# Statistics of two tiles at a time, biases carried in the weights' last row, and one gelu per block in a four-layer kernel

## The chip, the cores and the metric

The kernel runs on one core of a Trainium2 chip. The metric is device time in microseconds (us) for one launch; before the change it is 726.42 us, the median of three runs (725.71 to 728.25). A core has five engines that run their own instruction streams and wait for each other through semaphores: TensorE (PE in the profile, its weight loads PEld), VectorE (DVE), ScalarE (ACT), GpSimd (POOL) and SyncE (SP), which here only issues transfers.

## The reference

The input `u` has 8 sequences of 512 tokens with 128 features. Four layers follow each other, each on a layer norm without gain and bias, each added to its input:

```
x = x + L0_attn(ln(x))   # state-space scan; W_in, W_out divided by max(largest singular value, 1)
x = x + L0_ffn(ln(x))    # ln(x) @ W[idx] + b[idx], idx = argmax(log_softmax(logits) + gumbel(u))
x = x + L1_attn(ln(x))   # delta rule: 16 heads of 8 x 8 state, step by step over the tokens
x = x + L1_ffn(ln(x))    # experts

def L1_ffn(x, w_router, w1, b1, w2, b2):
    probs = softmax(x @ w_router)
    topk_w, topk_idx = top_k(probs, 2)          # two of eight experts
    h = gelu(x @ w1[i] + b1[i])                 # 128 -> 512, tanh form
    out = sum over the two of weight * (h @ w2[i] + b2[i])
```

All numbers are float32. A layer norm's output `(x - mean) / sqrt(var + eps)` sums to zero over the 128 features; the change makes use of it.

## The kernel before

The 4096 tokens are cut into 32 tiles of 128 rows (16 steps of each of the 8 sequences), and the tiles into eight groups of four (`SIZES`). For each group `first_layers` computes the scan (`scanned`, `ssm_out`) and the second layer (`linear`), `delta_in` the projections of the third layer, `delta_rule` its recurrence, and `route` the choice of experts. The experts run on bundles of 4, 8, 8, 8 and 4 tiles (`GROUPS`): `experts` sorts the tokens by expert with indexed transfers of GpSimd (`scatter`, line 1233, into `places`), reads them back in blocks of 128 rows (15 blocks for a bundle of 4 tiles, 23 for one of 8, 99 in all), applies both products of the block's expert, writes `results`, and gathers them back by index (line 1368).

`delta_rule` has four steps per tile, and each step six VectorE instructions that depend on one another (lines 1023 to 1037): a product over `kq`, a reduction of `so`, a product and a reduction with `tmat`, a product into `st` and its reduction, which is the state of the next step. `kq` is loaded by SP from DRAM (`scratch`), where `delta_in` has put q and k.

At the start `spectral` finds the largest singular values of `W_in` and `W_out` by squaring a matrix 24 times (two matrices side by side), with a scale from the trace at every third squaring; the results make `gain`, which `ssm_out` needs.

The places in the code that the change and the prediction touch:

- `moments` (line 722): for each tile a statistics instruction on VectorE (`bn_stats`, six numbers: count, mean and sum of squared deviations of the even elements and of the odd ones) and one that joins them (`bn_aggr`). It is called for the input (`input_statistics`, tile names ending in i) and in `linear` (a), `delta_in` (b) and `route` (e). `factors` (732) makes `rstd` and `shift` from it on GpSimd, with a power; `normalised` (749) applies them on ScalarE.
- `linear` (875): `x1b = x1 + bsel` on GpSimd, then `x2 = product + x1b` on VectorE. `wsel` and `bsel`, the chosen weights and bias, come by indexed transfers (710 to 719).
- `w1b_dram` (656 to 663): the experts' first weights with four more columns that hold the biases, made in DRAM by one transfer of `w1` and one of the columns; `rows` (509) gathers small vectors, the 32 rows of `b1` among them, which TensorE transposes into `cols`.
- `hidden_of` (1310): loads a block's weights (`load_weights`, 1274), four products into one PSUM bank (`ph`, two banks), and four gelus of 128 columns, each with its bias column.

Nothing is issued in the order of the text. `Recorder` notes every operation (so line 317 stands in the profile for nearly all), and `Plan.best` (184) works out an order for all engines by list scheduling: an operation gets a key (`nc.key`, in estimated us; `due(t)` is 15 t), a cost from `_cost` and a wait from `LAG`; `place` (210) starts on each engine, among the operations that are ready within 0.7 us, the one with the lowest rank, which is its key or, in a second turn, its latest start worked back from the end (`backward`). An operation that is ready while the engine has nothing else is started, however late its key. The order with the earliest estimated end among `DRAFTS` drafts with randomly moved keys is then issued; on the chip each engine follows it strictly. SP's transfers are among these operations: one that waits holds those behind it. Memory is handed out in turn: `ptile(shape, tag, bufs)` gives the next of a tag's buffers, so `"w1b"` (five buffers) serves `x` of the later groups at first and the experts' weights afterwards, and `"hid"` (three) the raw weights and then the hidden blocks.

Of the kernel before, what the change touches and what calls it, by code (L numbers as in the profile page):

```python
# [17 lines left out]
P = 128  # L18
# [6 lines left out]
NHB = 4  # L25
SQUARINGS = 24
FIRST = 9
# [313 lines left out]
def _cost(engine, name, n, kw):  # L341

    if engine == "tensor":
        return 0.2 if name == "transpose" else 0.22 + 0.0019 * max(_size(kw["rhs"])[1] - 96, 0)
    if engine == "vector":
        if name == "tensor_tensor_scan":
            return 0.1 + 0.0026 * n
        return 0.19 + 0.00103 * n + (0.2 if n == 9 * 32 else 0.0)
    if engine == "scalar":
        columns = sum(isinstance(kw.get(k), bass.AP) for k in ("bias", "scale"))  # L350
        return 0.18 + 0.00085 * n + (0.0, 0.0001 * n, 0.13)[columns]
    return 0.22 + 0.0015 * n if n < 64 else 0.4 + 0.0017 * n

# [3 lines left out]
BEHIND = 8.0  # L357
DRAFTS = 60
JITTER = 15
# [7 lines left out]
def seq_kernel(  # L367
# [72 lines left out]
    def ctile(shape, name, dtype=F32):  # L440
        return const.tile(shape, dtype, tag=name, name=name)
# [18 lines left out]

    WIDE = {"both": 2 * N, "xne": P, "w1b": NHB * P + NHB, "drive": N + B, "z": N + B, "kq": NR * QN, "prod": B * BL * BL}

# [4 lines left out]
    def stile(shape, tag, dtype=F32, bufs=2):  # L467
        return turn(
            "small_" + tag, bufs, lambda name: pipe.tile(shape, dtype, tag=name, name=name)
        )[tuple(slice(0, m) for m in shape)]  # L470
# [35 lines left out]

    R_BP, R_AL, R_DB, R_G, R_B, R_QKVB, R_B1 = 0, 3, 4, 5, 6, 7, 11
    n_rows = R_B1 + NE * NHB
    rows = ptile([n_rows, P], "hid", 3)
    nc.scalar.dma_start(rows[R_BP : R_BP + 3], bp.rearrange("(c p) -> c p", p=P))  # L510
    for r, v in ((R_AL, alpha_log), (R_DB, delta_bias), (R_G, ln_g), (R_B, ln_b)):
        nc.scalar.dma_start(rows[r : r + 1], v.rearrange("(c p) -> c p", p=P))
    nc.scalar.dma_start(rows[R_QKVB : R_QKVB + 4], b_qkvb.rearrange("(c p) -> c p", p=P))
    nc.scalar.dma_start(rows[R_B1:], b1.rearrange("e (c p) -> (e c) p", p=P))
    lg_col = ctile([P, 1], "lg_col")
# [10 lines left out]
    wr = ctile([P, NE], "wr")  # L526
    nc.sync.dma_start(wr, w_router)

    b2_sb = ctile([NT * NE, NT, D], "b2_sb")
# [122 lines left out]
    def col(r):  # L652
        return cols[:, r : r + 1]


    FW = NHB * P + NHB
    w1b_dram = dram.tile([NE * P, FW], F32, tag="w1b_dram", name="w1b_dram")
    nc.key = 0.0
    nc.sync.dma_start(w1b_dram[:, 0 : NHB * P], w1.rearrange("e d f -> (e d) f"))
    nc.sync.dma_start(  # L660
        w1b_dram[:, NHB * P :].rearrange("(e p) c -> p e c", p=P),
        cols[:, R_B1:].rearrange("p (e c) -> p e c", c=NHB),
    )

# [39 lines left out]
    w_row = ctile([P, 1], "w_row", U32)  # L704
    nc.vector.tensor_copy(w_row, pk[:, 4:5])
    b_row = ctile([P, 1], "b_row", U32)
    nc.vector.tensor_copy(b_row, topi[:, 0:1])
    wsel = ctile([P, D], "wsel")
    bsel = ctile([P, D], "bsel")
    for dst, src, row in (  # L710
        (wsel, ffn_W.rearrange("e d f -> (e d) f"), w_row),
        (bsel, ffn_b, b_row),
    ):
        nc.gpsimd.indirect_dma_start(
            out=dst[:, :],
            out_offset=None,
            in_=src,
            in_offset=bass.IndirectOffsetOnAxis(ap=row[:, :1], axis=0),
        )


    def moments(src, part, bufs=2):

        n = src.shape[1]
        st = stile([P, NT, 6], "st" + part)
        mv = stile([P, NT, 2], "mv" + part, F32, bufs)[:, 0:n]
        for i in range(n):
            nc.vector.bn_stats(st[:, i, :], src[:, i, :])
            nc.vector.bn_aggr(mv[:, i, :], st[:, i, :])
        return mv  # L730

    def factors(mv, part, norms=1, bufs=2):

        n = mv.shape[1]
        rstd = stile([P, norms, NT], "rstd" + part, F32, bufs)[:, :, 0:n]
        nc.gpsimd.tensor_scalar_add(rstd[:, 0], mv[:, :, 1], LN_EPS)
        if norms == 2:

            nc.gpsimd.tensor_scalar(rstd[:, 1], mv[:, :, 1], 1.0 + LN_EPS, LN_EPS * LN_EPS, ALU.mult, ALU.add)
        nc.gpsimd.tensor_tensor(rstd, rstd, mhalf[:, 0:norms, 0:n], ALU.pow)  # L740
        shift = stile([P, norms, NT], "shift" + part, F32, bufs)[:, :, 0:n]
        nc.gpsimd.tensor_mul(shift, mv[:, :, 0].unsqueeze(1).to_broadcast([P, norms, n]), rstd)
        nc.gpsimd.tensor_scalar_mul(shift, shift, -1.0)
        return rstd, shift
# [3 lines left out]

    def normalised(src, rstd, shift, xn, norm=0):
        for i in range(src.shape[1]):  # L750
            nc.scalar.activation(
                xn[i], src[:, i, :], AF.Identity, bias=shift[:, norm, i : i + 1], scale=rstd[:, norm, i : i + 1]
            )
        return xn

    def tiles_of(v):
        return [v[:, i, :] for i in range(v.shape[1])]
# [22 lines left out]
    def over_tiles(v, n):  # L780
        return v.unsqueeze(1).to_broadcast([P, n, D])
# [93 lines left out]
    def linear(x1):  # L875

        n = x1.shape[1]
        rstd, shift = statistics(x1, "a")
        xT = ptile([P, n * P], "f", FIRST)
        nc.scalar.copy(xT, transposed(normalised(x1, rstd, shift, tiles_of(ptile([P, n, D], "f", FIRST)))))  # L880
        x1b = ptile([P, n, D], "f", FIRST)
        nc.gpsimd.tensor_add(x1b, x1, over_tiles(bsel, n))
        x2 = ptile([P, n, D], "x2", 2)
        nc.vector.tensor_add(x2, tokens_out(xT, wsel), x1b)
        return x2
# [178 lines left out]
    def route(g, x3, group):  # L1064
# [3 lines left out]
        rstd, shift = statistics(x3, "e")  # L1068
        x3n = normalised(x3, rstd, shift, [ptile([P, D], "xne", MAXT) for _ in range(NT)])
        x3T = ptile([P, N], "x3T")  # L1070
# [94 lines left out]
    def experts(group):  # L1165
# [144 lines left out]
        def hidden_of(j):  # L1310
# [16 lines left out]
            for c in range(NHB):  # L1327
# [3 lines left out]
                )  # L1331
            for c in range(NHB):
                cs = slice(c * P, (c + 1) * P)
                nc.scalar.activation(
                    hid[:, cs], ph[:, cs], AF.Gelu_apprx_tanh, bias=w1b[:, NHB * P + c : NHB * P + c + 1]
                )
            return hid
# [66 lines left out]
    sp = ctile([P, 24], "sp")  # L1404
    smax, rmax, rtr, sums, lam, sig = (sp[:, i : i + 2] for i in (0, 2, 6, 8, 12, 14))
    nc.vector.tensor_reduce(smax, w_both, AX.X, ALU.max, apply_absolute_value=True)
# [13 lines left out]
    def spectral(i, copied, scaled):  # L1420

        c = slice(i, i + 1)
        junk = ptile([P, P], ("x3T", "fin")[i])

        def power():
            return ptile([P, P], ("xbT", "xne")[i], (2, MAXT)[i])

        def total(x, y, column):

            sums_ = part[:, 2 * column + i : 2 * column + i + 1]  # L1430
            if x is y:
                nc.scalar.activation(junk, x, AF.Square, accum_out=sums_)
            else:
                nc.vector.tensor_mul(junk, x, y)
                nc.vector.tensor_reduce(sums_, junk, AX.X, ALU.add)
            at = ph_tile()[:, 0:1]
            nc.tensor.matmul(
                at, lhsT=ones, rhs=part[:, 2 * column + i : 2 * column + i + 1], start=True, stop=True
            )
            return at  # L1440

        cur, a0 = power(), ptile([P, P], f"back{i}")
        scaled(cur, w_both[:, i, :], rmax[:, c])
        factor = None
        for step in range(SQUARINGS + 1):
            bank = po_tile()
            nc.tensor.matmul(bank[:, 0:P], lhsT=cur, rhs=cur, start=True, stop=True)
            if step % 3 == 0 and step < SQUARINGS:


                trace = total(cur, cur, 0)
                nc.vector.tensor_scalar_max(rtr[:, c], trace, 1e-18)
                nc.vector.reciprocal(rtr[:, c], rtr[:, c])
                nc.vector.tensor_mul(rtr[:, c], rtr[:, c], rtr[:, c])
            cur = a0 if step == 0 else power()
            if step % 3 == 1:
                scaled(cur, bank[:, 0:P], rtr[:, c])
            else:
                copied(cur, bank[:, 0:P])
            yield  # L1460
        nc.vector.tensor_copy(sums[:, c], total(cur, a0, 0))
        nc.vector.tensor_scalar_max(rtr[:, c], total(cur, ident, 1), TINY)
        nc.vector.reciprocal(rtr[:, c], rtr[:, c])
        yield

# [3 lines left out]
    for _ in zip(  # L1469
        spectral(0, nc.vector.tensor_copy, vector_scaled), spectral(1, nc.scalar.copy, nc.scalar.mul)  # L1470
    ):
        pass
    nc.vector.tensor_mul(lam, sums, rtr)
    nc.gpsimd.tensor_tensor(sig, lam, half, ALU.pow)
# [23 lines left out]
    for g in range(1, NG):  # L1498
# [4 lines left out]
        input_statistics(g, x)  # L1503

    x2s = {g: first_layers(g) for g in range(2)}
    for g in range(NG):
# [70 lines left out]
```

## Time and profile before

| | |
|---|---|
| median of three runs | 726.42 us |
| the profiled execution | 728.65 us |
| its span, first to last instruction | 726.9 us |
| mean granted TensorE clock | 0.832 |
| first step of the delta rule (`so`) | 105.35 us |
| first gelu of an expert block | 276.4 us |
| last bundle's places known (`dest`) | 642 us |
| last expert product on TensorE | 707.2 us |
| DMA traffic | 105.94 MB, 146 GB/s |

The page of the profile lists busy time by engine. As stages with different limits follow each other, tables by stretches of 20 us say more. Groups of instructions carry the names of the tiles they write and read (`out<-in`), their shape, count, busy time, mean duration, and the idle time ahead of them with what ended it. The page names DRAM tensors by their ends.

### The profile page before, as it was taken

Reading aid. Unit: us, or ns where it says so; the run is one execution under the profiler, and the core shown is the slowest. Engines: PE = TensorE matmul, PEld = TensorE weight load, DVE = VectorE, ACT = ScalarE, POOL = GpSimd, SP = SyncE. Lnnn points to the kernel's source line nnn. Section 1 sums busy time; section 2 is a strip of 40 time slices with the busy share of each in tenths; the row PEclk is TensorE's granted clock in tenths of the full one; section 3 lists DMA queues with packets and bytes.
Section 4 is the critical chain, followed back from the end, with each engine's and each line's share of the span. In section 5 each row is a group of like instructions: output and inputs, shape, how many; then the busy total and the mean of one; then the engine's idle time right before and its main releaser. Section 6 shows DMA issues by size and latency. Waiting matters only on the chain. (4 is left out here: it accounts for less than half of the span.)

```text
span 726.9 us, 11166 instructions
## 1 busy us (share of the span) xinstructions
PE 520.2 (72%) x2948; PEld 403.9 (56%) x2948; DVE 527.0 (73%) x1468; ACT 468.8 (64%) x1062; POOL 548.1 (75%) x681
## 2 busy tenths in 40 slices
PE   5885466576584288699558788883978887988890
PEld 4672124435353156368326577662857776888890
DVE  5775068998999799999959999995798998230013
ACT  3865747654692679998675987852675743675560
POOL 6667485694768899699868998978478878876454
PEclk9856566877699599889758889996899999999995
DMA  3734263233352564276456456565686786569662
GB/s 106 200 108 123 60 148 79 73 95 88 78 125 75 143 178 125 76 181 179 127 148 162 111 138 169 163 173 135 168 211 184 201 245 194 171 192 276 168 176 80
DMA packets 97717, 105.94 MB, mean 146 GB/s; under 512 B 9100, under 2 KB 72535, under 8 KB 97655
## 3 DMA queue, kind: packets, MB, share of 16 engines
q1 hardware_dynamic: 92992, 96.66, 49.2%
q0 software_dynamic: 4160, 8.53, 4.0%
q8 instruction: 25, 0.41, 0.3%
q14 instruction: 38, 0.30, 0.1%
q10 hardware_dynamic: 502, 0.03, 0.0%
HBM read 81.26 MB, written 23.94 MB: 145 GB/s over the span
## 5 line engine op out<-in xcount | busy, mean ns | idle before, releaser
L317 ACT ACTIVATE hid<-ph,w1b 128x128 f32<-128x128 f32 x396 | 113.4, 378 | 48.7 <-PE ph L317 23.4
L317 PE MATMUL ph<-xbT,w1b 128*128 128x128 f32 x792 | 118.3, 292 | 12.0 <-DMA w1b<-w1b_dram 5.4
L317 PEld LDWEIGHTS ph<-xbT,w1b 128*128 128x128 f32 x792 | 107.3, 205 | 26.4 <-issue 10.7
L317 DVE TENSOR_TENSOR so<-kq,st 128x512 f32<-128x512 f32 x128 | 87.5, 684 | 15.6 <-PE in L317 7.9
L317 POOL DMA_INDIRECT back<-results,small_dest x64 | 62.8, 982 | 33.0 <-issue 14.0
L317 DVE TENSOR_REDUCE st<-so 128x32 f32<-128x288 f32 x128 | 84.1, 657 | 3.5
L1297 PE MATMUL po<-w_sb,hid 128*128 x536 | 80.3, 288 | 7.2 <-ACT hid L317 4.0
L1297 PEld LDWEIGHTS po<-w_sb,hid 128*128 128x128 f32 x536 | 73.2, 204 | 15.7 <-issue 7.3
L1235 POOL DMA_INDIRECT places<-xne,small_dest x64 | 64.3, 1004 | 18.8 <-issue 13.7
L286 ACT ACT_TABLE_LOAD x52 | 66.7, 1283 | 6.2 <-DMA hid<-in_L_ffn_b_dram 5.4
L317 PE MATMUL po<-wo,so 128*128 128x128 f32 x256 | 45.0, 330 | 32.9 <-DVE so L317 14.8
L317 DVE TENSOR_REDUCE st<-st 128x64 f32<-128x320 f32 x128 | 63.6, 497 | 4.0
L317 PEld LDWEIGHTS po<-wo,so 128*128 128x128 f32 x256 | 41.3, 240 | 43.2 <-DVE so L317 16.1
L317 PE MATMUL in<-b,head_ones 128*128 128x512 f32 x80 | 50.6, 721 | 11.3 <-DVE x L317 3.6
L317 DVE TENSOR_TENSOR st<-kq,st 128x256 f32<-128x256 f32 x128 | 54.8, 428 | 4.2
L317 PE MATMUL in<-f,wT 128*128 128x512 f32 x64 | 44.5, 789 | 15.1 <-ACT qkp L317 5.4
L317 POOL TENSOR_TENSOR qkp<-qkp,upd 128x512 f32<-128x512 f32 x32 | 38.8, 1214 | 13.3 <-ACT upd L317 13.2
L317 PE MATMUL in<-b,wqkvb 128*128 128x512 f32 x64 | 40.5, 731 | 9.4 <-ACT beta L317 4.3
L317 DVE TENSOR_REDUCE st<-prod 128x32 f32<-128x128 f32 x128 | 37.6, 293 | 12.0 <-ACT upd L317 6.8
L317 POOL TENSOR_TENSOR so<-so 128x512 f32<-128x512 f32 x24 | 30.5, 1271 | 17.8 <-DVE so L317 17.7
L317 DVE SCALAR_TENSOR_TENSOR fin<-back,small_weight,fin 128x128 f32<-128x128 f32 x16 | 5.3, 353 | 51.5 <-DMA back<-results,small_dest 50.8
L317 DVE TENSOR_TENSOR prod<-tmat,st 128x128 f32<-128x128 f32 x128 | 36.6, 286 | 8.0 <-POOL tmat L317 3.5
(292 smaller groups left out, 1310.4 us busy)
## 6 DMA issues: line engine op xcount, KB each, us to landing
kq<-scratch SPq DMA_DIRECT2D x64, 512.0 KB
w1b<-w1b_dram SPq DMA_DIRECT2D x99, 258.0 KB
xb<-places SPq DMA_DIRECT2D x21, 256.0 KB
results<-yb SPq DMA_DIRECT2D x21, 256.0 KB
places<-yb SPq DMA_DIRECT2D x2, 1472.0 KB
x<-in_L_attn_u_dram SPq DMA_DIRECT2D x32, 64.0 KB
w1b_dram<-in_L_ffn_w_dram SPq DMA_DIRECT2D x1, 2048.0 KB
scratch<-qn SPq DMA_DIRECT2D x8, 256.0 KB
```

The lines of the kernel that those rows point to most:

```text
L286: self.hw.scalar.preload_act_table_set(switch)
L317: return method(*(on(x) for x in args), **{k: on(x) for k, x in kw.items()})
L1235: rows_out = hw.gpsimd.indirect_dma_start(out=table[0 : nblk * P, :], out_offset=bass.IndirectOffsetOnAxis(ap=at, axis=0), in_=src, in_off ...
L1297: return hw.tensor.matmul(out_.on(nc.banks), lhsT=src, rhs=w2_f[:, bass.ds(at + c * P, P)], start=(c == 0), stop=(c == NHB - 1),)
```

## The change

Five things are changed together.

1. `moments` uses one `bn_stats` for two tiles: the elements are taken in turn from both, so that the even ones are those of the first tile and the odd ones those of the second. `bn_aggr` goes; `factors` divides the sum of squared deviations by 128 itself.
2. As a layer norm's output sums to zero, `sum x_d W_d` equals the sum over the first 127 features with `W_d - W_127`; the last feature is set to 1 and the last row of the weights to the bias. So `normalised` writes 127 columns, a `memset` makes the last one 1, and the additions of `bsel` and of `b1` go. `wsel` and the router's weights become differences; the experts' weights are made in `fold_weights`: for each expert two loads, a subtraction on GpSimd and a store of 127 rows. A row of `w1b_dram` shrinks from 516 to 512 numbers.
3. Without a bias column, a block's gelu is one instruction over 512 columns.
4. In `spectral` there is one squaring less (23), the factor is applied twice in one instruction instead of being squared, and the end needs one sum of products and one of squares for each matrix.
5. The planner knows a cost for `memset` and makes 150 drafts instead of 60.

```diff
-SQUARINGS = 24
+SQUARINGS = 23
...
+    if name == "memset":
+        return 0.15 + 0.0008 * n
...
-DRAFTS = 60
+DRAFTS = 150
...
-    R_BP, R_AL, R_DB, R_G, R_B, R_QKVB, R_B1 = 0, 3, 4, 5, 6, 7, 11
-    n_rows = R_B1 + NE * NHB
+    R_BP, R_AL, R_DB, R_G, R_B, R_QKVB = 0, 3, 4, 5, 6, 7
+    n_rows = R_QKVB + 4
...
-    nc.scalar.dma_start(rows[R_B1:], b1.rearrange("e (c p) -> (e c) p", p=P))
...
+    wr_last = ctile([P, NE], "wr_last")
+    nc.sync.dma_start(wr_last, w_router[D - 1].partition_broadcast(P))
+    nc.gpsimd.tensor_sub(wr, wr, wr_last)
...
-    FW = NHB * P + NHB
+    FW = NHB * P
...
-    nc.sync.dma_start(w1b_dram[:, 0 : NHB * P], w1.rearrange("e d f -> (e d) f"))
-    nc.sync.dma_start(
-        w1b_dram[:, NHB * P :].rearrange("(e p) c -> p e c", p=P),
-        cols[:, R_B1:].rearrange("p (e c) -> p e c", c=NHB),
-    )
+    nc.sync.dma_start(w1b_dram.rearrange("(e p) f -> e p f", p=P)[:, D - 1, :], b1)
+
+    def fold_weights():
+
+        for e in range(NE):
+            nc.key = due(-3.0 + 0.8 * e)
+            w, last = ptile([P, FW], "w1b", 5), ptile([P, FW], "hid", 3)
+            nc.sync.dma_start(w, w1[e])
+            nc.sync.dma_start(last, w1[e, D - 1].partition_broadcast(P))
+            nc.gpsimd.tensor_sub(w, w, last)
+            nc.sync.dma_start(w1b_dram[e * P : (e + 1) * P - 1], w[0 : P - 1])
...
-    bsel = ctile([P, D], "bsel")
+    both_ = ptile([P, 2, D], "x3", 2)
+    wlast, bsel = both_[:, 0, :], both_[:, 1, :]
     for dst, src, row in (
         (wsel, ffn_W.rearrange("e d f -> (e d) f"), w_row),
+        (wlast, ffn_W.rearrange("e d f -> (e d) f"), last_row),
         (bsel, ffn_b, b_row),
     ):
...
+    nc.vector.tensor_sub(wsel, wsel, wlast)
+    nc.vector.scalar_tensor_tensor(wsel, bsel, ident[:, P - 1 : P], wsel, ALU.mult, ALU.add)
...
     def moments(src, part, bufs=2):
...
-        st = stile([P, NT, 6], "st" + part)
-        mv = stile([P, NT, 2], "mv" + part, F32, bufs)[:, 0:n]
-        for i in range(n):
-            nc.vector.bn_stats(st[:, i, :], src[:, i, :])
-            nc.vector.bn_aggr(mv[:, i, :], st[:, i, :])
+        mv = stile([P, NT, 3], "mv" + part, F32, bufs)[:, 0:n]
+        for i in range(0, n, 2):
+            nc.vector.bn_stats(
+                mv[:, i : i + 2].rearrange("p i s -> p (i s)"), src[:, i : i + 2, :].rearrange("p i d -> p d i")
+            )
...
-        nc.gpsimd.tensor_scalar_add(rstd[:, 0], mv[:, :, 1], LN_EPS)
+        nc.gpsimd.tensor_scalar(rstd[:, 0], mv[:, :, 2], 1.0 / P, LN_EPS, ALU.mult, ALU.add)
...
-    def normalised(src, rstd, shift, xn, norm=0):
+    def normalised(src, rstd, shift, xn, norm=0, width=D):
...
     def linear(x1):
...
-        nc.scalar.copy(xT, transposed(normalised(x1, rstd, shift, tiles_of(ptile([P, n, D], "f", FIRST)))))
-        x1b = ptile([P, n, D], "f", FIRST)
-        nc.gpsimd.tensor_add(x1b, x1, over_tiles(bsel, n))
+        xn = ptile([P, n, D], "f", FIRST)
+        nc.gpsimd.memset(xn[:, :, D - 1 : D], 1.0)
+        nc.scalar.copy(xT, transposed(normalised(x1, rstd, shift, tiles_of(xn), 0, D - 1)))
         x2 = ptile([P, n, D], "x2", 2)
-        nc.vector.tensor_add(x2, tokens_out(xT, wsel), x1b)
+        nc.vector.tensor_add(x2, tokens_out(xT, wsel), x1)
...
-            for c in range(NHB):
-                cs = slice(c * P, (c + 1) * P)
-                nc.scalar.activation(
-                    hid[:, cs], ph[:, cs], AF.Gelu_apprx_tanh, bias=w1b[:, NHB * P + c : NHB * P + c + 1]
-                )
+            nc.scalar.activation(hid, ph, AF.Gelu_apprx_tanh)
...
             if step % 3 == 1:
-                scaled(cur, bank[:, 0:P], rtr[:, c])
+                nc.vector.tensor_scalar(cur, bank, rtr[:, c], rtr[:, c], ALU.mult, ALU.mult)
             else:
-                copied(cur, bank[:, 0:P])
+                copied(cur, bank)
             yield
-        nc.vector.tensor_copy(sums[:, c], total(cur, a0, 0))
-        nc.vector.tensor_scalar_max(rtr[:, c], total(cur, ident, 1), TINY)
+        bank = po_tile()[:, 0:P]
+        nc.tensor.matmul(bank, lhsT=a0, rhs=cur, start=True, stop=True)
+        nc.vector.tensor_scalar_max(rtr[:, c], squares(cur), TINY)
         nc.vector.reciprocal(rtr[:, c], rtr[:, c])
+        nc.vector.tensor_mul(a0, cur, bank)
+        nc.vector.tensor_reduce(part[:, 2 + i : 3 + i], a0, AX.X, ALU.add)
+        nc.vector.tensor_mul(lam[:, c], rtr[:, c], summed(1))
...
+    for x in [ptile([P, D], "xne", MAXT) for _ in range(MAXT)]:
+        nc.gpsimd.memset(x[:, D - 1 : D], 1.0)
...
+    fold_weights()
     x2s = {g: first_layers(g) for g in range(2)}
```

`squares(x)` is ScalarE's square with a running sum followed by `summed(0)`, and `summed(column)` the product with ones that adds the 128 partial sums.

More of the change, by code (lines that the diff above doesn't have):

```diff
@@ L459, in turn @@
         return slots[tag][at % bufs]
-    WIDE = {"both": 2 * N, "xne": P, "w1b": NHB * P + NHB, "drive": N + B, "z": N + B, "kq": NR * QN, "prod": B * BL * BL}
+    WIDE = {"both": 2 * N, "xne": P, "w1b": NHB * P, "drive": N + B, "z": N + B, "kq": NR * QN, "prod": B * BL * BL}
     def ptile(shape, tag, bufs=1, dtype=F32):
@@ L512, in seq_kernel @@
         nc.scalar.dma_start(rows[r : r + 1], v.rearrange("(c p) -> c p", p=P))
-    nc.scalar.dma_start(rows[R_QKVB : R_QKVB + 4], b_qkvb.rearrange("(c p) -> c p", p=P))
-    nc.scalar.dma_start(rows[R_B1:], b1.rearrange("e (c p) -> (e c) p", p=P))
+    nc.scalar.dma_start(rows[R_QKVB:], b_qkvb.rearrange("(c p) -> c p", p=P))
     lg_col = ctile([P, 1], "lg_col")
@@ L705, in seq_kernel @@
     nc.vector.tensor_copy(w_row, pk[:, 4:5])
+    last_row = ctile([P, 1], "last_row", U32)
+    nc.vector.tensor_scalar(last_row, pk[:, 3:4], float(D), D - 1.0, ALU.mult, ALU.add)
     b_row = ctile([P, 1], "b_row", U32)
@@ L735, in factors @@
         rstd = stile([P, norms, NT], "rstd" + part, F32, bufs)[:, :, 0:n]
-        nc.gpsimd.tensor_scalar_add(rstd[:, 0], mv[:, :, 1], LN_EPS)
+        nc.gpsimd.tensor_scalar(rstd[:, 0], mv[:, :, 2], 1.0 / P, LN_EPS, ALU.mult, ALU.add)
         if norms == 2:
-            nc.gpsimd.tensor_scalar(rstd[:, 1], mv[:, :, 1], 1.0 + LN_EPS, LN_EPS * LN_EPS, ALU.mult, ALU.add)
+            nc.gpsimd.tensor_scalar(rstd[:, 1], mv[:, :, 2], (1.0 + LN_EPS) / P, LN_EPS * LN_EPS, ALU.mult, ALU.add)
         nc.gpsimd.tensor_tensor(rstd, rstd, mhalf[:, 0:norms, 0:n], ALU.pow)
         shift = stile([P, norms, NT], "shift" + part, F32, bufs)[:, :, 0:n]
-        nc.gpsimd.tensor_mul(shift, mv[:, :, 0].unsqueeze(1).to_broadcast([P, norms, n]), rstd)
+        nc.gpsimd.tensor_mul(shift, mv[:, :, 1].unsqueeze(1).to_broadcast([P, norms, n]), rstd)
         nc.gpsimd.tensor_scalar_mul(shift, shift, -1.0)
@@ L747, in statistics @@
         return factors(moments(src, part), part, norms)
-    def normalised(src, rstd, shift, xn, norm=0):
+    def normalised(src, rstd, shift, xn, norm=0, width=D):
         for i in range(src.shape[1]):
             nc.scalar.activation(
-                xn[i], src[:, i, :], AF.Identity, bias=shift[:, norm, i : i + 1], scale=rstd[:, norm, i : i + 1]
+                xn[i][:, 0:width],
+                src[:, i, 0:width],
+                AF.Identity,
+                bias=shift[:, norm, i : i + 1],
+                scale=rstd[:, norm, i : i + 1],
             )
@@ L1068, in route @@
         rstd, shift = statistics(x3, "e")
-        x3n = normalised(x3, rstd, shift, [ptile([P, D], "xne", MAXT) for _ in range(NT)])
+        x3n = normalised(x3, rstd, shift, [ptile([P, D], "xne", MAXT) for _ in range(NT)], 0, D - 1)
         x3T = ptile([P, N], "x3T")
@@ L1404, in seq_kernel @@
     sp = ctile([P, 24], "sp")
-    smax, rmax, rtr, sums, lam, sig = (sp[:, i : i + 2] for i in (0, 2, 6, 8, 12, 14))
+    smax, rmax, rtr, lam, sig = (sp[:, i : i + 2] for i in range(0, 10, 2))
     nc.vector.tensor_reduce(smax, w_both, AX.X, ALU.max, apply_absolute_value=True)
@@ L1426, in power, with summed @@
             return ptile([P, P], ("xbT", "xne")[i], (2, MAXT)[i])
[L1428 to L1435, printed above, removed]
+        def summed(column):
             at = ph_tile()[:, 0:1]
@@ L1440, in total, with squares @@
             return at
+        def squares(x):
+            nc.scalar.activation(junk, x, AF.Square, accum_out=part[:, i : i + 1])
+            return summed(0)
         cur, a0 = power(), ptile([P, P], f"back{i}")
         scaled(cur, w_both[:, i, :], rmax[:, c])
-        factor = None
         for step in range(SQUARINGS + 1):
[L1446 to L1452, printed above, removed]
+            bank = po_tile()[:, 0:P]
+            nc.tensor.matmul(bank, lhsT=cur, rhs=cur, start=True, stop=True)
+            if step % 3 == 0:
+                nc.vector.tensor_scalar_max(rtr[:, c], squares(cur), 1e-18)
                 nc.vector.reciprocal(rtr[:, c], rtr[:, c])
-                nc.vector.tensor_mul(rtr[:, c], rtr[:, c], rtr[:, c])
             cur = a0 if step == 0 else power()
             if step % 3 == 1:
-                scaled(cur, bank[:, 0:P], rtr[:, c])
+                nc.vector.tensor_scalar(cur, bank, rtr[:, c], rtr[:, c], ALU.mult, ALU.mult)
             else:
-                copied(cur, bank[:, 0:P])
+                copied(cur, bank)
             yield
-        nc.vector.tensor_copy(sums[:, c], total(cur, a0, 0))
-        nc.vector.tensor_scalar_max(rtr[:, c], total(cur, ident, 1), TINY)
+        bank = po_tile()[:, 0:P]
+        nc.tensor.matmul(bank, lhsT=a0, rhs=cur, start=True, stop=True)
+        nc.vector.tensor_scalar_max(rtr[:, c], squares(cur), TINY)
         nc.vector.reciprocal(rtr[:, c], rtr[:, c])
+        nc.vector.tensor_mul(a0, cur, bank)
+        nc.vector.tensor_reduce(part[:, 2 + i : 3 + i], a0, AX.X, ALU.add)
+        nc.vector.tensor_mul(lam[:, c], rtr[:, c], summed(1))
         yield
@@ L1472, in seq_kernel @@
         pass
-    nc.vector.tensor_mul(lam, sums, rtr)
+    for x in [ptile([P, D], "xne", MAXT) for _ in range(MAXT)]:
+        nc.gpsimd.memset(x[:, D - 1 : D], 1.0)
     nc.gpsimd.tensor_tensor(sig, lam, half, ALU.pow)
```

## The prediction

> **What bounds the kernel now.** The listing of cores comes first: one core, span 726.9 us, mean granted TensorE clock 0.832. The execution took 728.65 us, so 1.75 us lie around the span; it is 2.2 us above the median of the three runs (726.42). I work out a difference in the trace and take it from the median.
>
> The page's busy times show no engine full over the whole span:
>
> ```profile
> PE 520.2 (72%) x2948; PEld 403.9 (56%) x2948; DVE 527.0 (73%) x1468; ACT 468.8 (64%) x1062; POOL 548.1 (75%) x681
> ```
>
> The table of stretches (length, then busy us and count for PE, PEld, DVE, ACT, POOL, then clock, DMA share, GB/s) separates three stages:
>
> ```profile
> 80.00:100.00 20.00, 14.54 (x19) 4.47 (x20) 3.18 (x3) 14.78 (x25) 12.01 (x12) 0.50 0.41 98
> ...
> 260.00:280.00 20.00, 17.42 (x102) 12.53 (x101) 18.48 (x58) 17.98 (x35) 19.04 (x28) 1.00 0.66 178
> ...
> 400.00:420.00 20.00, 15.21 (x71) 10.53 (x71) 18.76 (x50) 18.32 (x38) 19.17 (x26) 0.84 0.42 114
> ...
> 640.00:660.00 20.00, 18.26 (x149) 18.27 (x150) 2.82 (x15) 13.55 (x44) 13.93 (x14) 0.91 0.69 198
> ```
>
> To 105 us a single chain runs through all engines, each of which waits. From 105 to about 620 VectorE works 18.5 of every 20 us on the delta rule, and ScalarE and GpSimd are nearly as full in places. From 614 on TensorE is full with the experts' blocks of the last two groups, and the last 20 us are the way out. The second stage is VectorE's because its own waits there are few; these four are 21.5 us of all 28.6 between 105 and 620:
>
> ```profile
> DVE so L317 <- PE in L317: 7.9, 1, 7.9
> DVE st L317 <- ACT upd L317: 6.8, 2, 3.9
> DVE prod L317 <- POOL tmat L317: 3.5, 1, 3.5
> DVE x L317 <- PE in L317: 3.3, 2, 3.0
> ```
>
> The groups by shape give durations (mean ns after the busy time):
>
> ```profile
> L317 ACT ACTIVATE hid<-ph,w1b 128x128 f32<-128x128 f32 x396 | 113.4, 378 | 48.7 <-PE ph L317 23.4 <-issue 16.3 <-ACT hid L317 3.8
> L317 DVE TENSOR_REDUCE st<-so 128x32 f32<-128x288 f32 x128 | 84.1, 657 | 3.5
> L317 DVE TENSOR_REDUCE st<-st 128x64 f32<-128x320 f32 x128 | 63.6, 497 | 4.0
> L317 DVE BATCH_NORM_STATS2 small_sta<-x 128x6 f32<-128x128 f32 x32 | 8.6, 268 | 0.2
> L317 DVE BATCH_NORM_AGGREGATE small_mva<-small_sta 128x2 f32<-128x6 f32 x32 | 5.8, 181 | 1.1
> ```
>
> **Moments.** A group of four tiles now needs four statistics and four aggregates; in the timeline of group 1 they hold VectorE from 107.30 to 108.91, 0.80 us a pair of tiles. Afterwards a pair is one instruction over 256 elements that takes its elements in turn from two tiles 512 bytes apart. The trace has no such instruction. Reading in a row, the reductions of 128 elements (0.293 us) and of 320 (0.497) put 256 at 0.43; the reduction of `so`, whose neighbours also lie 512 bytes apart, takes 0.657 for 288, thus 1.8 ns an element and 0.60 for 256. A worse stride is at hand on ScalarE: `tmat`, written 20 bytes apart, takes 1148 ns where 512 elements in a row take 628, 1.0 ns more an element, which would make 0.69. With 0.03 us to the next instruction a pair costs 0.46, 0.63 or 0.72, and saves 0.34, 0.17 or 0.08. I take 0.17, since the engine and the 512 bytes are those of `so`. Of 48 pairs outside the input statistics (8 groups x 3 x 2), four stand in the first stage, two after the last tile, 42 in VectorE's stage: 42 x 0.17 = 7.1 us (ends 3.4 and 14.3). The 16 pairs of the input fall into VectorE's idle time before 65 us and count nothing; without that cover they would be 2.7.
>
> [...]
>
> **The first stage.** The spectral loop's `xbT` copies start at 10.69 and 51.94 with 24 steps between: 1.72 us a step, and one step goes. After the last copy come 5.1 us to the end of `lam` (57.08): four products and four reductions on VectorE at a pitch of 0.33, and four sums on TensorE. Half of the products and reductions go (4 x 0.33 = 1.3 us), a matrix product of 0.8 comes: -0.5. The 16 multiplications of the factor go too; some are long:
>
> ```profile
> 26.00 2.83 DVE L317 TENSOR_TENSOR sp<-sp 128x1 f32<-128x1 f32 x1
> ...
> 59.43 0.73 DVE L317 SCALAR_TENSOR_TENSOR x<-in,gain,x 128x512 f32<-128x512 f32 x1
> ...
> 61.56 1.27 POOL L317 TENSOR_TENSOR f<-x,bsel 128x512 f32<-128x512 f32 x1
> 62.79 0.24 POOL L317 TENSOR_SCALAR small_rstda<-small_mva 128x4 f32<-128x4 f32 x1
> ```
>
> The first of them is 2.7 us over its usual 0.16 and holds up the copy behind it; TensorE shows 1.9 idle there, and I count 1.5. Together `gain` is 3.7 earlier. What it is multiplied with is ready at 55.7, 3.7 before the line at 59.43, so the whole just fits. Next, the sum with `bsel` runs at 61.56 ahead of `small_rstda`, whose moments were ready at 61.9: -0.9. Four pairs at 0.17: -0.7. Against it: a `memset` of a column for each group and eight for `xne` (some 0.2 each by GpSimd's short rows, beside the chain), one more gather by index (0.96 like `wsel`'s, around 25 us and needed at 68), and the eight subtractions of the experts' weights (1.27 each by GpSimd's 512-element rows, 10.2 in all). GpSimd waits some 22 us between 42 and 107, so these fit; one caught at the wrong moment costs 1.3. Sum -4.0 (ends -6 and 0).
>
> **The experts' weights.** One transfer from DRAM to DRAM (2 MB) and one of the biases go; `b1` into `w1b_dram`, `wr_last` and, for each expert, two loads of 256 KB and a store of 127 rows come: 26 issues on SP, at about 0.43 us, 11 us, while SP issues nothing from 44 to 60 and from 69 to 89. The result is needed only by the first expert block, whose gelu starts at 276. But each store waits for GpSimd's subtraction, and behind it in SP's order stand `x` of group 1 (60.2), `scratch<-qn` (89.8) and `kq<-scratch` (92.4), for which the first delta block waits. Of the 92,992 packets of that queue the trace's packet list has 5,408 of four bytes for 386 transfers: 290 x 16 + 96 x 8, and 96 have eight as the outermost count on one side (`u`, `out`, `b2`). [...] 127 rows of 2 KB at the 85 to 114 ns of such packets are 0.7 to 0.9 us spread over 16 engines, 10.8 to 14.5 on one. Eight stores are then 6 or 86 to 116 us on the first engine. [...] What counts is what waits behind: with stores apart from the `scratch` and `kq` transfers the cost is a few us of slack (the first `kq` pair is there at 98.4, used at 105.35), and their keys (-45 to 39 against -78 for `scratch`) put them behind wherever both are ready. I take +1 (ends 0 and +41, worked out as a rival).
>
> [...]
>
> **Gelu, and GpSimd.** Four gelus hold ScalarE 113.4/99 = 1.15 us a block; one over 512 elements, with no column, is like the copies from PSUM (`xbT<-ph`, 592 ns): 54 us less for ScalarE in all, under VectorE and TensorE. The additions of `bsel` free 7 x 1.27 = 8.9 us of GpSimd after 105. Both reach the path only through the waits shown above, 21.5 us; a new order of all instructions can also bring new ones, one of the size of the largest (7.9). I take -4 (ends -18 and +8). In the last stage the second product waits for all of the gelu (0.6) instead of a quarter (0.38), but TensorE has the next block's first product and the second bank meanwhile; a shorter hold of the banks speaks for a gain: -1 (ends -4 and +2). The last 20 us are unchanged.
>
> Sum: -7.1 - 4.0 + 1 - 4 - 1 = -15.1: 713.5 for the profiled execution, 711.3 from the median, say 711. What is saved before 577, where group 3 is routed, moves the start of the full last stage; TensorE has gaps until 540 to follow.
>
> **Rivals.** *The stores hold the first delta rule* (slower). If GpSimd's gaps draw all eight stores ahead of `scratch<-qn`, the first engine, busy from about 48 on, is free at 48 + 8 x 11.3 = 138, and a transfer issued at 89.8 ends 48 us later: less 7 us of slack, +41. With five ahead it is +7. The middle, +24, gives 711 - 1 + 24 = 734; from 16 us on the kernel is slower. For it speaks the list of packets, and SP's free time before 89; against it the keys. *The new order eats the savings*: moments at 0.72 (-3.4), +4 of new waits, the first stage -1: about 726, no difference. For it: 21.5 us of waits that depend on order alone. *The contiguous price holds and the waits go*: -14.3 - 5 - 10 - 2 gives 695. For it: both GpSimd and ScalarE above 18 of 20 at 260 and 400; against it `so`.
>
> **How the numbers follow.** Forecast 0.52 (own range 701 to 722), contiguous 0.20, stores 0.19, no difference 0.09. A measurement here tells 0.3% (2.2 us) from no change. Faster: 0.52 + 0.20 + 0.02 from the stores + 0.02 from the last = 0.76; same 0.05; slower 0.19. Below 693 I leave 0.06, above 742 some 0.09.
>
> **What would show it.** One statistics instruction per pair near 600 ns (430 or 690 for the ends); VectorE's busy time less by 10 us or more; `gain` used near 56 and the first `so` near 101; gelu near 600 ns x99; no idle VectorE before the first `so` that ends on a DMA of `kq`. A wait there of over 7 us would make the prediction wrong, as would a sum of VectorE's waits from 105 on above 40 us.

## The result

The changed kernel takes 764.12 us (median; 762.89 to 774.47), the one before 727.34 in the same runs: ratio 1.050, 95% interval 1.046 to 1.054. It is slower by 5%; the prediction was 711 us, with a range to 742 and 0.76 for faster. Medians are of all runs; the ratios and intervals here and below are worked out apart from them, on the fast runs alone (without the one of 774.47 us, whose clock was 0.816 against 0.829 to 0.834), and can differ from the quotient of two medians by up to 0.4%.

The profiled execution after has a span of 762.2 us at a clock of 0.832, 35.3 more than before. Three marks of VectorE's timeline divide it:

| | before | after | difference |
|---|---|---|---|
| start to the first `so` of the delta rule | 105.35 | 159.39 | +54.0 |
| first to last `so` | 511.5 | 486.4 | -25.1 |
| last `so` to the end | 110.0 | 116.4 | +6.4 |
| span | 726.9 | 762.2 | +35.3 |

The loss lies ahead of the delta rule, and a third of it (18.7 us) is won back behind. The first mark flatters the kernel before a little: its first `so` runs ahead of VectorE's last preparations, and the reduction that follows comes only at 110.03 (after: 160.11), so counted from there the delay is 50 us, and 4 of the 25.1 us belong to the mark. The table of stretches of the changed kernel (columns as before: length, PE, PEld, DVE, ACT, POOL, clock, DMA share, GB/s):

```profile
80.00:100.00 20.00, 7.85 (x10) 2.23 (x10) 0.00 (x0) 11.99 (x23) 6.51 (x10) 0.50 0.31 95
100.00:120.00 20.00, 0.00 (x0) 0.00 (x0) 0.00 (x0) 0.00 (x0) 1.68 (x2) 0.50 0.12 41
120.00:140.00 20.00, 13.25 (x29) 5.70 (x30) 13.60 (x17) 10.84 (x19) 19.26 (x21) 0.74 0.07 27
140.00:160.00 20.00, 3.80 (x14) 2.39 (x14) 0.61 (x1) 4.99 (x8) 1.37 (x2) 0.60 0.59 144
160.00:180.00 20.00, 6.84 (x30) 5.46 (x30) 18.66 (x41) 7.00 (x14) 6.20 (x8) 0.59 0.32 73
```

From 100 to 120 no engine computes but GpSimd for 1.7 us, and the DMA engines are at 0.12: nothing is scarce, everything waits. In the kernel before the delta rule was running from 105.35 on. What SP does in that time, from its timeline (start, time in the issue, transfer, count):

```profile
42.58 0.27 SPq L317 DMA_DIRECT2D w1b_dram<-w1b  x1
...
82.90 0.28 SPq L317 DMA_DIRECT2D w1b_dram<-w1b  x1
...
98.23 0.64 SPq L317 DMA_DIRECT2D w1b_dram<-w1b  x1
98.96 9.96 SPq L317 DMA_DIRECT2D w1b<-in_L_ffn_w_dram  x1
109.01 20.83 SPq L317 DMA_DIRECT2D w1b_dram<-w1b  x3
129.93 10.05 SPq L317 DMA_DIRECT2D scratch<-qn  x1
...
149.44 1.21 SPq L317 DMA_DIRECT2D kq<-scratch  x2
```

The stores `w1b_dram<-w1b` are those of 127 rows. Once the first are under way, an issue that is done in some 0.4 us elsewhere can take 10, whatever it issues: a load of weights (98.96), one of the three stores at 109.01 (20.83 together), `scratch<-qn` (129.93; 0.36 before). All eight stores stand ahead of `scratch`, and `kq` follows only at 149.44. From 112 to 140 us the trace's packet list shows almost nothing but one packet of 2 KB at a time, one every 80 ns: 127 of them are 10.2 us. The DMA share is 0.07 there, about one engine of 16. And the queue's packets of four bytes are now 5,664: 5,408 less two transfers of 16, plus 17 loads of 16, `b1` with 8, and eight stores with one each. Single ones come at 127.98, 138.15 and 148.31, 10.2 us apart. VectorE's timeline has the consequence:

```profile
60.13 0.75 DVE L317 SCALAR_TENSOR_TENSOR x<-in,gain,x 128x512 f32<-128x512 f32 x1 [0.46 <-POOL gain L317]
...
120.84 0.69 DVE L317 TENSOR_TENSOR drive<-f,in 128x512 f32<-128x512 f32 x1 [49.20 <-POOL f L317]
...
138.63 1.35 DVE L317 TENSOR_TENSOR tmat<-b,beta 128x128 f32<-128x128 f32 x1
159.39 0.69 DVE L317 TENSOR_TENSOR so<-kq,st 128x512 f32<-128x512 f32 x1 [19.41 <-DMA kq<-scratch]
```

`gain` is used at 60.13 (before: 59.43), the product into `drive` then waits for GpSimd until 120.84 (before: 92.99), and the first `so` for the load of `kq`. GpSimd in turn had waited, at its last subtraction, for the load that SP issued at 98.96:

```profile
118.32 1.26 POOL L317 TENSOR_TENSOR w1b<-w1b,hid 128x512 f32<-128x512 f32 x1 [18.87 <-DMA w1b<-in_L_ffn_w_dram]
```

So the delay falls into two parts. VectorE's preparations (the last `tmat`) end at 139.98 instead of 110.12, 30 us later, behind GpSimd; then come 19.4 us of waiting for `kq`. The groups by shape, in answer to those of before:

```profile
L317 ACT ACTIVATE hid<-ph 128x512 f32<-128x512 f32 x99 | 58.3, 597 | 72.6 <-PE ph L317 62.7 <-PE po L1319 6.6 <-PE in L1319 2.9
...
L317 DVE TENSOR_REDUCE st<-so 128x32 f32<-128x288 f32 x128 | 84.2, 658 | 3.4
...
L317 POOL TENSOR_TENSOR w1b<-w1b,hid 128x512 f32<-128x512 f32 x8 | 10.1, 1262 | 41.3 <-DMA w1b<-in_L_ffn_w_dram 27.3 <-DMA hid<-in_L_ffn_w_dram 12.6 <-DMA w1b_dram<-in_L_ffn_b_dram 1.4
...
L317 DVE BATCH_NORM_STATS2 small_mva<-x 128x6 f32<-128x256 f32 x16 | 6.1, 423 | 0.2
```

The gelu fell from 113.4 to 58.3 us, and two tiles' statistics take 423 ns where 2 x (268 + 181) stood. The subtractions take 10.1 us as counted, but GpSimd was idle 41.3 us ahead of them, nearly all of it until loads landed: in its order the critical chain's instructions stand behind.

### The profile page after: what moved, and what is told of

Same layout as the page of the kernel before. It is cut to its first block, busy times and chain, and to the rows that moved or that the text cites. A ratio compares the mean times of both kernels' runs of the same rounds, so it can differ in the third digit from the quotient of the medians.

```text
span 762.2 us, 10669 instructions
## 1 busy us (share of the span) xinstructions
PE 506.4 (66%) x2948; PEld 399.6 (52%) x2948; DVE 508.5 (67%) x1265; ACT 420.9 (55%) x763; POOL 550.1 (72%) x699
## 5 line engine op out<-in xcount | busy, mean ns | idle before, releaser
L317 PE MATMUL ph<-xbT,w1b 128*128 128x128 f32 x792 | 113.8, 288 | 15.4 <-ACT xbT L317 6.7
L317 PEld LDWEIGHTS ph<-xbT,w1b 128*128 128x128 f32 x792 | 104.5, 202 | 28.5 <-issue 12.9
L317 DVE TENSOR_TENSOR so<-kq,st 128x512 f32<-128x512 f32 x128 | 87.8, 686 | 38.5 <-DMA kq<-scratch 19.4
L317 ACT ACTIVATE hid<-ph 128x512 f32<-128x512 f32 x99 | 58.3, 597 | 72.6 <-PE ph L317 62.7
L317 PE MATMUL po<-wo,so 128*128 128x128 f32 x280 | 51.2, 343 | 50.6 <-DVE so L317 30.9
L317 PEld LDWEIGHTS po<-wo,so 128*128 128x128 f32 x280 | 47.3, 250 | 63.8 <-DVE so L317 33.8
L1257 POOL DMA_INDIRECT places<-xne,small_dest x64 | 63.5, 992 | 18.7 <-issue 13.8
L317 PE MATMUL in<-b,head_ones 128*128 128x512 f32 x80 | 48.2, 693 | 20.8 <-ACT vals L317 4.9
L317 PE MATMUL in<-f,wT 128*128 128x512 f32 x64 | 38.5, 693 | 7.9 <-DVE x L317 4.1
L317 POOL TENSOR_TENSOR w1b<-w1b,hid 128x512 f32<-128x512 f32 x8 | 10.1, 1262 | 41.3 <-DMA w1b<-in_L_ffn_w_dram 27.3
```

What stands on the lines that cost most here:

```text
L317: return method(*(on(x) for x in args), **{k: on(x) for k, x in kw.items()})
L1257: rows_out = hw.gpsimd.indirect_dma_start(out=table[0 : nblk * P, :], out_offset=bass.IndirectOffsetOnAxis(ap=at, axis=0), in_=src, in_off ...
```

## The experiments

The experiments ran on three chips. The kernel before took 729.1 us on the first (cut stores, whole stores, ScalarE's stores, moments alone), 728.2 on the second (moments as before, four gelus, subtractions on VectorE, another seed) and 774.9 on the third (the added stores, the spectral loop, no differences), so ratios are compared across chips, and of the third only marks early in the trace. "Stage" is the time from first to last `so`.

**Stores cut in two**, of 112 rows and of 15:

```diff
-            nc.sync.dma_start(w1b_dram[e * P : (e + 1) * P - 1], w[0 : P - 1])
+            nc.sync.dma_start(w1b_dram[e * P : e * P + 112], w[0:112])
+            nc.sync.dma_start(w1b_dram[e * P + 112 : (e + 1) * P - 1], w[112 : P - 1])
```

> [...] Theory stores (one engine takes all 127 rows, its queue fills and SP is held): the first so comes back from 159.4 to between 98 and 108, no issue on SP of 10 us, time 700 to 716. Rival loads (the sixteen loads of 256 KB, half of them 128 readings of one row, and the subtractions that wait for them on GpSimd): the first so stays above 140 and the time above 745. Rival order (the new order of instructions lost the time): above 745 too, with no held issue to explain it.

708.52 us, ratio 0.974 (0.969 to 0.979): some 56 us less than the changed kernel by this edit, with the same bytes, loads and subtractions. First `so` at 106.16, stage 493.9. SP's timeline of this kernel:

```profile
43.90 1.33 SPq L317 DMA_DIRECT2D w1b_dram<-w1b  x3
...
81.36 3.25 SPq L317 DMA_DIRECT2D w1b_dram<-w1b  x6
90.55 0.40 SPq L317 DMA_DIRECT2D scratch<-qn  x1
92.87 1.21 SPq L317 DMA_DIRECT2D kq<-scratch  x2
```

The last six pieces need 3.25 us of issuing, and `scratch` and `kq` go out in 0.4 to 0.6 us each; the longest issue of a piece is 5.23 us (at 64.33). The loads are out as the main cause. The planner makes a new order with every edit, this one too; but in all six kernels, here and below, that cut the stores or make them whole the first `so` stands between 103 and 110, so a lucky order is out as well. But `gain` is used at 62.39, later than in either kernel; GpSimd's timeline has a reason, and ScalarE's shows who waits for it:

```profile
37.74 2.50 POOL L317 TENSOR_TENSOR w1b<-w1b,hid 128x512 f32<-128x512 f32 x2 [5.72 <-DMA b_sb<-in_L_ffn_b_dram]
40.20 2.34 POOL L317 TENSOR_TENSOR both<-both,f 128x1024 f32<-128x1024 f32 x1
...
42.57 1.15 ACT L317 ACTIVATE both<-both,tiny_col 128x1024 f32<-128x1024 f32 x1 [7.45 <-POOL both L317]
```

GpSimd had been idle 5.72 us before 37.74, waiting for transfers, and only then came to `both`. ScalarE waits 7.45 us for it, and in ScalarE's order the spectral loop's next copy stands behind (43.62).

**One store of 128 rows**, with the bias already in row 127 of the tile:

```diff
-            nc.sync.dma_start(w1b_dram[e * P : (e + 1) * P - 1], w[0 : P - 1])
+            nc.sync.dma_start(w[P - 1 : P], b1[e : e + 1])
+            nc.sync.dma_start(w1b_dram[e * P : (e + 1) * P], w)
```

> The changed kernel, b1 of the expert loaded into row 127 of the tile in SBUF, and one store of 128 rows. Theory stores: like the cut store, first so 98 to 108, time 700 to 716. Rivals loads and order: above 745.

721.14 us, 0.991 (0.988 to 0.994); first `so` at 103.39, as by the theory, though the time missed the stated 700 to 716. The stage is even shorter than with the cut stores (483.6), but from the last `so` to the end it is 131.6 against 107.0: another order of nearly the same work.

**The stores issued by ScalarE**, still of 127 rows:

```diff
-            nc.sync.dma_start(w1b_dram[e * P : (e + 1) * P - 1], w[0 : P - 1])
+            nc.scalar.dma_start(w1b_dram[e * P : (e + 1) * P - 1], w[0 : P - 1])
```

> The changed kernel, the stores of 127 rows issued by ScalarE instead of SP. They still run on one engine. If the damage is that SP's own queue fills and holds what is behind, the loads and kq are free of it: first so 100 to 115, time 702 to 724, unless ScalarE is held in SP's place, which its issues of 10 us would show. If a full first engine is enough, kq waits there: first so above 125, time above 735. Rival loads: above 745.

751.56 us, 1.035 (1.030 to 1.040); first `so` at 147.8. ScalarE's timeline shows its own issues held:

```profile
75.57 20.29 ACTq L317 DMA_DIRECT2D w1b_dram<-w1b  x2
...
110.20 8.75 ACTq L317 DMA_DIRECT2D w1b_dram<-w1b  x2
```

and SP's shows that its loads are held too, although the stores are no longer in its queue:

```profile
75.00 12.91 SPq L317 DMA_DIRECT2D x<-in_L_attn_u_dram  x4
92.57 13.88 SPq L317 DMA_DIRECT2D hid<-in_L_ffn_w_dram  x3
```

So it isn't SP's queue alone: while the stores run, issues are held on ScalarE and on SP alike. Four loads of `u` took 2.71 us to issue in the kernel before (at 60.23). The time and the first `so` are within what was stated for this case (above 735 and above 125).

**Eight stores added to the kernel before**, of 127 and of 128 rows (`%d`), from `wqkvb` into a tensor that nothing reads:

```diff
+    for e in range(NE):
+        nc.key = due(-3.0 + 0.8 * e)
+        nc.sync.dma_start(spare[e * P : e * P + %d], wqkvb[0:%d])
```

> The kernel before and, added to it, eight stores of 127 rows (2 KB each) from `wqkvb` into a spare DRAM tensor that nothing reads, with the keys of the change's stores; no loads, no subtractions. Theory stores: each takes some 10 us on one engine (127 x 80 ns), SP is held in its issues, and the loads behind them come late: first so at 112 to 160 instead of 105, time 733 to 780. Rival (it took the loads and the subtractions together with them): within 724 to 733.

> The same with eight stores of 128 rows. Theory stores: sixteen engines, under 1 us each, no held issue of 5 us on SP that the kernel before has not; first so at 100 to 110, time 722 to 734, the spread being that of a new order. Rival (2 MB more traffic at the start is what costs): like the stores of 127 rows.

With 127 rows 828.92 us, ratio 1.071 (1.064 to 1.078), 54 us; first `so` at 163.36, even later than the stated 112 to 160. With 128 rows 774.24, ratio 1.001 (0.997 to 1.005); first `so` at 106.16. The issues on SP, 127 rows:

```profile
38.37 67.97 SPq L317 DMA_DIRECT2D spare<-wqkvb  x8
106.45 12.62 SPq L317 DMA_DIRECT2D w1b<-in_L_attn_u_dram  x3
```

and 128 rows:

```profile
38.20 7.18 SPq L317 DMA_DIRECT2D spare<-wqkvb  x8
```

One row less in each store, and eight issues take 68.0 us instead of 7.2. No loads of weights and no subtractions are in this, so the stores alone can cost as much as the changed kernel lost. The wait that does it is another one, though. Here the stores stand ahead of the last input tiles, whose statistics stand ahead of the rest in VectorE's order:

```profile
125.33 0.29 DVE L317 BATCH_NORM_STATS2 small_sti<-w1b 128x6 f32<-128x128 f32 x1 [61.80 <-DMA w1b<-in_L_attn_u_dram]
```

`scratch` then goes out at 145.95 in 0.36 us and nothing waits long for `kq`. That both kernels lose about 54 us is therefore a coincidence of size; that held issues cost tens of microseconds, and that one more row per store removes them, is not.

**Moments alone**, in the kernel before:

> The kernel before with the statistics of two tiles by one instruction alone. With the 0.424 us that the changed kernel's trace shows for it, 42 pairs in VectorE's stage save 0.80 - 0.46 = 0.34 each: 14 us, time 708 to 718. Rival order: a new order brings new waits and the time stays within 720 to 732.

720.22 us, 0.990 (0.987 to 0.993): 9 us less, short of the expected 14 and just inside the rival's 720 to 732. The stage is 499.0, 12.5 less than before (4 of them by the mark, as above), with 34.9 us of waits on VectorE in it against 28.6; 9.8 are lost again between the last `so` and the end (119.8). First `so` at 100.81.

**Cut stores, moments as before:**

> The kernel with the cut stores, but the statistics of each tile by its own two instructions as before. Theory moments: VectorE's stage (first to last so) grows from 493.9 by 42 x 0.34 = 14 us and most of it reaches the end: time 716 to 724 against 708.5. Rival order: the time moves by less than 5, or the other way.

723.62 us, ratio 0.993 (0.990 to 0.996) against 0.974 with the joint statistics: 1.9%, 14 us, as stated. As another order alone can make 1% (last experiment), the stage is the better witness: 511.6 against 493.9, 17.7 us longer, and 492.7 to 496.7 in the three other kernels with cut stores.

**Cut stores, four gelus per block** (without bias columns):

> The kernel with the cut stores, but four gelus of 128 columns for each block, without bias columns. Theory off the path: ScalarE is busier by 40 us or more and the time stays within 704 to 714. Rival ScalarE sets the pace in places: the waits of VectorE on what ScalarE makes grow and the time is 716 to 726.

710.49 us, 0.975 (0.970 to 0.979): no difference from 0.974, within the stated 704 to 714. The group's line:

```profile
L317 ACT ACTIVATE hid<-ph 128x128 f32<-128x128 f32 x396 | 80.8, 289 | 65.6 <-PE ph L317 52.7 <-PE po L1320 10.7 <-PE in L1320 0.7
```

A gelu of 128 columns without a bias column takes 289 ns, with one it took 378. Neighbours overlap, so busy time falls less: 80.8 us for the 396 against 113.4 in the kernel before. ScalarE is therefore busier by 23.1 us only (80.8 against 57.7 with one gelu per block), not the 40 expected, and this had no effect that shows.

**Cut stores, subtractions on VectorE:**

> The kernel with the cut stores, and the eight subtractions of the experts' weights and the router's on VectorE instead of GpSimd. Theory: GpSimd, which runs its instructions in order, stood waiting for the loads of the weights (5.7 us before 38) and held `both` and with it the spectral loop for 7 us; on VectorE, idle for long stretches before 105, gain comes at 54 to 58 instead of 62.4, the first so at 98 to 103, time 700 to 707. Rival: VectorE is then the one that waits in order and holds the loop itself: gain at 60 or later, time 706 to 714.

718.70 us, 0.985 (0.983 to 0.987). The rival's mechanism was right, though the time missed its 706 to 714 too: now VectorE waits in its order for the loads,

```profile
34.18 1.44 DVE L317 TENSOR_TENSOR w1b<-w1b,hid 128x512 f32<-128x512 f32 x1 [3.84 <-DMA w1b<-in_L_ffn_w_dram]
...
64.43 0.75 DVE L317 SCALAR_TENSOR_TENSOR x<-in,gain,x 128x512 f32<-128x512 f32 x1 [0.90 <-POOL gain L317]
```

3.84 us before 34.18, and `gain` is used at 64.43, later still.

**Spectral loop alone**, in the kernel before:

> The kernel before with the change of the spectral loop alone. Theory: without the weights' subtractions in GpSimd's order the loop shows its saving: gain used at 55 to 57 instead of 59.4, first so at 100 to 103, time 720 to 727. Rival: the loop saves nothing (the scaling of both matrices on VectorE costs what the step brings): gain at 59 or later, time 725 to 733.

Ratio 0.996 (0.992 to 1.000); VectorE's timeline:

```profile
55.58 0.75 DVE L317 SCALAR_TENSOR_TENSOR x<-in,gain,x 128x512 f32<-128x512 f32 x1 [0.90 <-POOL gain L317]
...
99.84 0.68 DVE L317 TENSOR_TENSOR so<-kq,st 128x512 f32<-128x512 f32 x1
```

`gain` is used 3.9 us earlier than before, as expected, and the first `so` is 5.5 earlier, just ahead of the stated 100 to 103 (on the same chip the kernel with added stores of 128 rows has them at 59.27 and 106.16, much like the kernel before); the end shows little of it.

**No differences for the experts' and the router's weights** (the experts' first biases are left out; `w1` goes to DRAM in one transfer):

> The changed kernel without differences for the experts' and the router's weights: w1 goes to DRAM in one transfer as before, no loads and subtractions, x normalised over all 128 columns; the experts' first biases are left out. Theory: what the weights' differences still cost beside the stores (GpSimd waiting for loads) goes too: gain at 54 to 57, first so at 97 to 101, time 698 to 708, at or below the cut stores' 708.5. Rival order: 708 to 720.

Ratio 0.964 (0.956 to 0.972), 28.8 us below the kernel before on that chip; the expected times were stated for a faster chip. First `so` at 101.89, `gain` used at 57.55, each under 1 us later than stated. Against the cut stores' 0.974 (0.969 to 0.979) the intervals overlap narrowly: what the differences still cost there is about 1%, no more than another order makes, and not settled.

**Cut stores, another seed of the planner:**

> The kernel with the cut stores, its planner's drafts drawn from another seed: the same instructions in another order. Theory order: of two kernels with nearly the same work (708.5 and 721.1) the difference is the order's, so this one lies more than 4 us from 708.5, on either side (probably 710 to 722). Rival: the order matters little and the time is 705 to 712.

716.65 us, 0.984 (0.982 to 0.987) against 0.974 (0.969 to 0.979): the same instructions in another order are 1% slower. Differences of 1% between the kernels above are therefore no proof of anything in the edit.

## Why the prediction was wrong

**The step that failed is the price of the stores.** The prediction took +1 us for "the experts' weights", with the ends 0 and +41, because the stores' keys "put them behind wherever both are ready". They were not ready together: the planner starts what is ready while an engine has nothing else, so the stores went out from 42.58 on and all eight stood ahead of `scratch<-qn` at 129.93. The other half of the step was the price of an issue, "about 0.43 us": the trace of before had one of 8.54 us on SP (at 29.27, a load into `w_sb` behind the 2 MB transfer from DRAM to DRAM). The mechanism stood there as the slower rival, with the count of four-byte packets for it, 0.19, and a middle of +24. The term measured +54.0 to the first `so` (50 to the reduction behind it), and cutting the stores took some 56 us off the end. The sign that the prediction had named came too: a wait for `kq` of over 7 us, which was 19.4. The rival's own sum was too low by a quarter: it had only the backlog on one DMA engine (+41). What it lacked is that the issuing engine stands still with each issue (10 us), so that loads come late too, and that in GpSimd's order the subtractions wait for these loads (41.3 us of idle time) with the scan's and the delta rule's instructions behind them. On the path this is 30 us of later preparations and 19.4 us of waiting for `kq`. How much would be left if only one of the two were mended was not tried.

No run shows over which DMA engines a transfer is spread: that a store of 127 rows stays on one, from which the +41 is worked out, was the author's estimate. What the runs show is, in the changed kernel, rows 80 ns apart, 10.2 us a store, at a DMA share of 0.07 of 16 engines, and with the added stores 68.0 us for eight issues of 127 rows against 7.2 for eight of 128.

**Moments: right mechanism, wrong size.** Taken: 0.60 us for a pair by the row of `so`, saving 0.17; measured 0.424, and 0.385 from one to the next, saving 0.42. 42 x 0.42 = 17.6 us instead of 7.1, and the stage with the old statistics is 17.7 longer. The 512 bytes between neighbours cost next to nothing here: 0.424 is what the reductions put for 256 elements in a row (0.43, interpolated; no run has this instruction over 256 in a row). Why the reduction of `so` takes 657 ns is open; it was not tried.

**The first stage.** The loop's part (-3.7) is right alone (3.9). The whole term (-4.0) did not arrive: with the cut stores the first `so` is 0.8 later than before. In the changed kernel `gain` was 0.7 later: the price of an unlucky subtraction was taken as its duration, 1.3 us, but an engine that runs in order waits for the transfers ahead of it first, 5.7 us with the cut stores.

**Gelu and GpSimd (-4).** VectorE's waits between the first and the last `so` add up to 28.6 us before, 27.1 with the cut stores, 29.6 with four gelus and 34.4 with the other seed. No gain of 4 us stands out of what the order makes, and the gelu has no visible part.

**The last stage (-1)**: +6.4 after, -3.0 with the cut stores, +21.6 with whole stores, +9.8 with the moments alone. Cut and whole stores do nearly the same work here and differ by 24.6 us, so most of this goes with the order, and the terms of the sum had no room for it. Without the stores' delay the sum was close, but in part by luck: 711 was said and the cut stores give 708.5, with 10.5 us more from the moments than said, 4.8 less from the first stage, and an order that with another seed is some 8 us slower.

## What to carry to other kernels

Look at the outermost count of each transfer: with a row less, 127 for 128, eight stores took 68.0 us to issue instead of 7.2 and cost 54 us; with two pieces of 112 and 15 rows, or with 128 rows, the delay was gone (first `so` at 106.16 and 103.39 instead of 159.39). A transfer that nobody needs for 200 us is not free if it goes ahead of one that somebody needs: a late deadline doesn't hold it back in a queue that runs in order (here all eight stores went out ahead of `scratch<-qn` at 129.93). When an edit makes a planner reorder everything, test two orders of the same work before a difference of 1% is put down to the edit.

## What the runs showed that was not expected

While stores of 127 rows run, the issuing instruction itself is held, on SP (up to 10 us each) and on ScalarE (20.29 us for two), and so are the issues of a queue that has none of the stores (12.91 us for four loads). One statistics instruction over 256 elements from two tiles takes 0.424 us, where two over 128 take 0.27 each and two joining instructions 0.18 each. A gelu of 128 columns takes 378 ns with a bias column and 289 without.
